# Deferred first loads, a fourth buffer for transposed inputs, and later normalization-factor transfers in a one-core transformer block

## The chip, the cores and the metric

The kernel runs on one core of one Trainium2 chip. The metric is device time in microseconds (us): the median of three runs. A profiled execution of the same program is used to see where the time goes; its span is the time from the first to the last instruction on the core.

## The reference

Sixteen sequences of 256 tokens with 256 channels, all float32, go through one pre-norm block: attention with 16 heads of 16 channels, then a gated feed-forward layer whose weights are interpolated from control points.

```python
x = x + attn(layernorm(x), wq, wk, wv, wo)
x = x + ffn(layernorm(x), gate_cp, up_cp, down_cp)

# attn: q, k, v = x @ w.T, split in 16 heads
scores = q k^T / sqrt(16); scores = -inf where j - i > 16
out = softmax(scores) v;   return out @ wo.T
# ffn: the weights are Catmull-Rom splines through 2033 control points each
return (silu(x @ gate_w.T) * (x @ up_w.T)) @ down_w.T
```

A query therefore sees every earlier token and 16 later ones.

## The kernel before

**Engines and order.** The kernel writes the order of the instructions of each engine out by hand: the wrapper `InOrder` (line 78) keeps each engine's queue in program order. TensorE (PE) multiplies, VectorE (DVE) takes maxima, products and statistics, ScalarE (ACT) exponentials and copies, GpSimd (POOL) masks and the power of -1/2. Nearly all transfers are issued by SyncE (SP), whose queue is in order too: an issue that waits for a buffer, an operand or an earlier transfer holds up every issue behind it. ACT issues the loads of the weights and, for batch 0, half of `spread`.

**A pipeline over the batches.** The loop at line 694 has 20 steps, s = 0 to 19. In step s, batch s-1 gets the maxima of its scores (`nb`), batch s-2 its exponentials and values (`tb`), batch s-3 the division, output projection and second normalization (`ob`), and batch s-4 most of its feed-forward layer. A step is cut into seven gaps, between which the scores of four head groups run (`inner` for groups 0 to 3 of the larger part, `outer` for the rest). `fill` puts feed-forward work in the gaps, `project` the work for a batch ahead: from step 4 on by a fixed rule, in steps 0 to 3 by the dictionary `early`, whose key is (step, gap) and whose value lists stages with their batch. In these steps the feed-forward weights are also made: `part` i builds one half of gate, up or down from `cp_in`, `tab_in` and `second_in`, and `keep_running` n issues n multiplications of the identity that nothing uses.

**The stages of a batch b that matter here.**

- `load_x(b)` and `load_xT(b)` load the batch's input as tokens by channels and as channels by tokens. x has ten buffers (pool `sbx`), xT three (`sb3`), each released after `project_v(b)`.
- `stats_a(b)` gives the factor 1/std of every token in `rstda`, 128 partitions by 2. `send_factors(b)` writes it to DRAM (`ra<-rstda`, 1 KB); `spread_factors(b)` reads it back to all partitions (`fa<-ra`, 128 KB), and so waits until the first has landed. Below they are ra(b) and fa(b).
- `project_qk(b)` multiplies xT by wq and wk into two PSUM buffers of the pool `ps_m`, which has two; DVE multiplies by fa(b) into `qkc`, which frees them. `spread(b)` lays qkc out over partitions by heads with eight transfers (`qk<-qkc`, 64 KB each). Batch 0 is normalized beforehand and needs no factors.
- `project_v(b)` does the same for the values, with `rstda` as ACT's scale.
- `turn_max(b)` sends the maxima of the scores to a row of qk with four transfers (`qk<-mxT`), which the scores for the exponentials need in the next step.
- `gather(b)` and `invert(b)` take the softmax sums and the heads back (`den<-au`, `ac<-au`), invert the sums on DVE (`rec`) and spread the inverses through DRAM (`rd<-rec`, `rb<-rd`).

**Initial loads.** Lines 139 to 158 issue, on SP, x0, x1, tab_in, cp_in 0, x2, xT1, second_in, cp_in 1, xT2, x3 and cp_in 2, and on ACT wq, wk, wv and wo. In every step lines 703 to 706, between gaps 1 and 2, issue x of batch s+4 and xT of batch s+3 (x4 and xT3 in step 0).

Of the kernel before, what the change touches and what calls it, by code (L numbers as in the profile page):

```python
# [11 lines left out]
F32 = mybir.dt.float32  # L12
# [6 lines left out]
P = 128  # L19
B, S, DIM = 16, 256, 256  # L20
# [73 lines left out]
def block_kernel(  # L94
# [14 lines left out]
    pe, dve, act, pool, sp = (  # L109
        InOrder(tc, e) for e in (nc.tensor, nc.vector, nc.scalar, nc.gpsimd, nc.sync)  # L110
    )

    const = ctx.enter_context(tc.tile_pool(name="const", bufs=1))
    sb = ctx.enter_context(tc.tile_pool(name="sb", bufs=2))
    sb1 = ctx.enter_context(tc.tile_pool(name="sb1", bufs=1))
    sb3 = ctx.enter_context(tc.tile_pool(name="sb3", bufs=3))
    sb4 = ctx.enter_context(tc.tile_pool(name="sb4", bufs=4))
# [10 lines left out]
    def load_x(b):  # L128
        xs[b] = sbx.tile([P, 2, DIM], F32, tag="x", name=f"x{b}")
        sp.dma_start(xs[b], x[b].rearrange("(c p) d -> p c d", p=P))  # L130


    xTs = {}

    def load_xT(b):
        xTs[b] = sb3.tile([P, 2, S], F32, tag="xT", name=f"xT{b}")
        sp.dma_start(xTs[b], xT[b].rearrange("(kc p) t -> p kc t", p=P))

    AHEAD = 2
    load_x(0)  # L140
    w_in = {}
    for nm, src in (("q", wqT), ("k", wkT), ("v", wvT), ("o", woT)):
        t = const.tile([P, 2, DIM], F32, tag=f"w{nm}", name=f"w{nm}")
        act.dma_start(t, src.rearrange("(kc p) o -> p kc o", p=P))
        w_in[nm] = t
    load_x(1)
    tab_in = const.tile([P, NPART + 2 * P], F32, tag="tab", name="tab_in")
    sp.dma_start(tab_in, tab)
    cp_in = const.tile([P, 3, NPART], F32, tag="cp", name="cp_in")
    second_in = const.tile([P, 2, NROW], mybir.dt.uint8, tag="second", name="second_in")  # L150
    sp.dma_start(cp_in[:, 0, :], cps[0])
    load_x(2)
    load_xT(1)
    sp.dma_start(second_in, second)
    sp.dma_start(cp_in[:, 1, :], cps[1])
    load_xT(2)
    load_x(3)
    sp.dma_start(cp_in[:, 2, :], cps[2])


    ident = const.tile([P, P], F32, tag="ident", name="ident")
# [53 lines left out]
    def normed(b, nm, tag):  # L215
        mv, rstd = moments.pop((b, nm))
        xn = sb.tile([P, 2, DIM], F32, tag=f"xn{tag}", name=f"xn{nm}{b}")
        for c in range(2):
            dve.tensor_scalar(
                xn[:, c, :], xs[b][:, c, :], mv[:, c, 0:1], rstd[:, c : c + 1],  # L220
                ALU.subtract, ALU.mult,
            )
        return xn

    def transposed(src, dst, nm):

        pt = ps_m.tile([P, 2, S], F32, tag="m", name=f"p{nm}")
        for kc in range(2):
            for c in range(2):
                pe.transpose(  # L230
                    pt[:, kc, c * P : (c + 1) * P],
                    src[:, c, kc * P : (kc + 1) * P],
                    ident,
                )
        act.copy(dst, pt)
# [6 lines left out]


    def norm_first():
        xTs[0] = sb3.tile([P, 2, S], F32, tag="xT", name="xT0")
        transposed(normed(0, "a", "f"), xTs[0], "ta0")

    sums = {}
# [119 lines left out]
    def inner(nb, tb, g):  # L368
        has_n, has_t = 0 <= nb < B, 0 <= tb < B
        qn, qt = qks[nb % NQK], qks[tb % NQK]  # L370
        if has_n:
            if g == 0:
                mxs[nb] = sb.tile([P, 2, H], F32, tag="mx", name=f"mx{nb}")
            scores(qn, True, g, P, S, P + HB + LOOK)
        if has_t:
            scores(qt, False, g, HB, HB - LOOK, S - HB + LOOK)
        if has_n:
            scores(qn, True, g, P + HB, S, S)
        if has_t:
            scores(qt, False, g, 0, 0, S)  # L380
        def exponentials(pr):
            e = sb6.tile([P, 2, S], F32, tag="e0", name=f"e0{tb}_{g}_{pr}")
            act.activation(e, tiles[pr][:, :, 0:S], AF.Exp, scale=HD**-0.5)

            pool.affine_select(
                out=e[:, :, 0:M0], in_=e[:, :, 0:M0],
                compare_op=ALU.is_ge, fill=0.0, base=LOOK,
                pattern=[[0, 2], [1, M0]], channel_multiplier=-1,
            )
            es[tb, 0, g, pr] = e  # L390

        def maxima(pr):
            for r in (2 * pr, 2 * pr + 1):
                find_max(nb, g, r, 1, S, S)

        read(exponentials if has_t else None, maxima if has_n else None)
# [205 lines left out]
    def do(stage, b, *args):  # L602
        if 0 <= b < B:
            stage(b, *args)
# [8 lines left out]
    def fill(s, gap):  # L613


        alone = s > B
        late = s >= B - AHEAD
        for what, at in (
            ((gate_up, s - 4, 1), 1),
            ((gate_up, s - 4, 2), 2 if late else 3),  # L620
            ((gate_up, s - 4, 3), 3 if late else 4),
            ((down, s - 4, 0), 4 if alone else 5),
            ((down, s - 4, 1), 5 if alone else 6),
            ((gate_up, s - 3, 0), 7),
        ):
            if at == gap:
                do(*what)
# [4 lines left out]
    def part(i):  # L632
# [7 lines left out]
        ),  # L640
        (0, 6): (
            (project_v, 0), (sum_weights, "v"), (center, "k"), (center, "v"), (keep_running, 1),
            (spread_factors, 1), (send_factors, 2), (spread_factors, 2),
        ),
        (1, 1): ((part, 0), (coefficients, 1)),
        (1, 2): ((project_qk, 1), (spread, 1)),
# [2 lines left out]
        (1, 5): ((keep_running, 2), (part, 2)),  # L649
        (1, 6): ((keep_running, 5), (project_v, 1)),  # L650
        (1, 7): (
            (stats_a, 3), (send_factors, 3), (spread_factors, 3), (keep_running, 4),
            (project_v, 2), (keep_running, 1),
        ),
        (2, 1): ((part, 3), (stats_a, 4), (send_factors, 4), (scores_and_values, 4)),
        (2, 2): ((project_qk, 3), (spread, 3), (spread_factors, 4)),
        (2, 3): ((keep_running, 6), (part, 4)),
        (2, 5): ((keep_running, 1), (part, 5)),
        (2, 6): ((keep_running, 4), (project_v, 3)),
        (2, 7): ((stats_a, 5), (send_factors, 5), (spread_factors, 5), (project_qk, 4)),  # L660
        (3, 1): ((stats_a, 6),),
        (3, 2): ((spread, 4), (project_qk, 5), (spread, 5), (send_factors, 6)),
        (3, 3): ((keep_running, 5), (project_v, 4)),
        (3, 4): ((spread_factors, 6),),
        (3, 6): ((keep_running, 4), (project_v, 5)),
    }
# [1 line left out]
    def project(s, gap):  # L668
        if s < 4:
            for stage, what in early.get((s, gap), ()):  # L670
                stage(what)
            return
        pb = s + AHEAD
        for stage, b, at in (
            (stats_a, pb + 1, 1),
            (project_qk, pb, 2),
            (spread, pb, 2),
            (send_factors, pb + 1, 2),
            (spread_factors, pb + 1, 4),
            (project_v, pb, 6),  # L680
        ):
            if at == gap:
                do(stage, b)
# [7 lines left out]
    stats_a(0)  # L691
    sum_weights("q")
    norm_first()
    for s in range(B + 4):
        nb, tb, ob = s - 1, s - 2, s - 3
        inner(nb, tb, 0)
        do(values, ob, 1)
        do(gather, ob)
        project(s, 1)
        fill(s, 1)  # L700
        inner(nb, tb, 1)
        do(invert, ob)
        if s + 2 + AHEAD < B:
            load_x(s + 2 + AHEAD)
        if 3 <= s + 1 + AHEAD < B:
            load_xT(s + 1 + AHEAD)
        project(s, 2)
        fill(s, 2)
        outer(nb, tb, 0)
        project(s, 3)  # L710
        fill(s, 3)
        inner(nb, tb, 2)
        do(values, tb, 0)
        project(s, 4)
        do(divide, ob)
        fill(s, 4)
        inner(nb, tb, 3)
        do(project_o, ob)
        do(stats_f, ob)
        project(s, 5)  # L720
        fill(s, 5)
        do(norm_f, ob)
        outer(nb, tb, 1)
        fill(s, 6)
        if s == 3:
            project(s, 6)
        do(turn_f, ob)
        if s != 3:
            project(s, 6)
        do(turn_max, nb)  # L730
        project(s, 7)
        fill(s, 7)
# [30 lines left out]
```

## Time and profile before

| | |
|---|---|
| median of three runs | 707.67 us (706.46 to 708.76) |
| the profiled execution: time, and span | 708.78 us, 707.0 us |
| mean granted TensorE clock | 0.958 |
| PE busy | 669.8 us, 95% of the span |
| DVE busy | 368.9 us, 52% |
| ACT busy | 208.2 us, 29% |
| POOL busy | 126.9 us, 18% |
| moved by DMA | 35.56 MB, mean 50 GB/s |

The page of the profile divides the span into 40 slices and gives each engine's busy share in tenths, the TensorE clock that was granted, and the load of the 16 DMA engines. The view of waits tells for how long an engine (or SP's queue) stood still and what ended it. The timeline lists start, duration and name of the instructions in order of time, with "x8" for eight merged ones. The table of stretches gives busy times, clock and DMA load between two times. All operations are recorded at one line, 88, so they are told apart by the names of their tiles, out<-in; batch numbers are left out and follow from the order.

### The profile page before, as it was taken

The numbers are of one execution on the slowest core, as the hardware profiler recorded it, in microseconds if no ns is written. First come the engines' busy times: TensorE is split into PE (matmuls) and PEld (weight loads), VectorE is DVE, ScalarE is ACT, GpSimd is POOL, SyncE is SP. The second block draws the span as 40 slices with busy tenths as digits, with TensorE's granted clock in tenths as the row PEclk, the third lists the DMA queues.
The fourth block names the chain that finished last, engine by engine and source line by source line (L and its number), as shares of the span: only waits on it lengthen the run. The fifth ranks groups of instructions, "written<-read, shape, count | busy, mean of one in ns | idle before, by whom it ended". The sixth has DMA issues, their size and how long they took to land.

```text
span 707.0 us, 18506 instructions
## 1 busy us (share of the span) xinstructions
PE 669.8 (95%) x7422; PEld 518.4 (73%) x7422; DVE 368.9 (52%) x1479; ACT 208.2 (29%) x368; POOL 126.9 (18%) x251
## 2 busy tenths in 40 slices
PE   7695997799999999999999999999999999999998
PEld 7363575478777777778787877777787777777777
DVE  5363455364665656465646566564637474633332
ACT  1021332232323333333323232333333233332210
POOL 5101221121121211121112111121212121211000
PEclk9695797799999999999999999999999999999999
DMA  9323505122131313141312214131201010100100
GB/s 256 46 51 45 76 4 110 30 73 43 39 63 32 79 33 85 27 91 26 85 32 69 48 24 77 31 67 33 54 19 33 20 30 25 27 26 24 40 22 16
DMA packets 44741, 35.56 MB, mean 50 GB/s; under 512 B 12400, under 2 KB 44016, under 8 KB 44656
## 3 DMA queue, kind: packets, MB, share of 16 engines
q1 hardware_dynamic: 43248, 33.07, 21.2%
q10 hardware_dynamic: 1408, 1.31, 1.2%
q8 instruction: 59, 0.97, 0.7%
q14 instruction: 26, 0.21, 0.2%
HBM read 16.78 MB, written 4.47 MB: 30 GB/s over the span
## 4 chain that ended last, share of the span: by engine, by line
PE 82%; DMA 2%; ACT 1%; SPq 1%; DVE 1%; issue 0%; ACTq 0%; DVEq 0%
PE pg L88 17%; PE pd L88 16%; PE pu L88 15%; PE scores L88 13%; PE po L88 6%; PE py L88 4%; PE pq L88 3%; PE pv L88 3%; PE pk L88 3%; SPq L88 1%; DMA ra<-rstda 1%; PE ptf L88 1%; ACT e L88 1%; DMA qk<-mxT 1%; ACT x2T L88 0%
## 5 line engine op out<-in xcount | busy, mean ns | idle before, releaser
L88 ACT ACTIVATE e<-scores 128x512 f32<-128x512 f32 (+1 forms) x192 | 117.7, 616 | 313.3 <-PE scores L88 238.2
L88 DVE CUSTOM_DVE_ANT_0 z<-scores,mask 128x144 bf16<-128x144 f32 (+1 forms) x512 | 154.5, 362 | 68.7 <-PE scores L88 60.3
L88 POOL TENSOR_SCALAR_AFFINE_SELECT e<-e 128x224 f32<-128x224 f32 (+1 forms) x192 | 93.3, 487 | 448.6 <-ACT e L88 448.2
L88 PE MATMUL scores<-qk 17*64 17x144 f32 (+7 forms) x4096 | 113.8, 329 | 21.5 <-DMA qk<-mxT 10.4
L88 PE MATMUL pg<-x2T,gateT 128*128 128x256 f32 x512 | 127.4, 392 | 2.9 <-ACT x2T L88 2.8
L88 PE MATMUL pu<-x2T,upT 128*128 128x256 f32 x512 | 121.8, 381 | 0.0
L88 PEld LDWEIGHTS scores<-qk 17*64 17x64 f32 (+1 forms) x4096 | 72.1, 135 | 61.9 <-issue 38.5
L88 PE MATMUL pd<-downT,inter 128*128 128x256 f32 x512 | 117.0, 382 | 0.0
L88 DVE SCALAR_TENSOR_TENSOR th<-th,pg 128x512 f32<-128x512 f32 x64 | 44.0, 688 | 132.3 <-ACT th L88 132.3
L88 PEld LDWEIGHTS pg<-x2T,gateT 128*128 128x128 f32 x512 | 93.1, 191 | 24.1 <-DVE mx L88 5.0
L88 PEld LDWEIGHTS pu<-x2T,upT 128*128 128x128 f32 x512 | 98.0, 191 | 13.6
L88 PEld LDWEIGHTS pd<-downT,inter 128*128 128x128 f32 x512 | 96.1, 190 | 14.0 <-issue 0.2
L88 ACT ACTIVATE th<-pg 128x512 f32<-128x512 f32 x64 | 38.3, 598 | 70.6 <-PE pg L88 70.2
L88 DVE TENSOR_TENSOR inter<-th,pu 128x512 f32<-128x512 f32 x64 | 44.1, 689 | 26.9 <-PE pu L88 26.9
L88 PE MATMUL po<-e,v 128*32 128x256 f32 (+1 forms) x1024 | 54.0, 355 | 0.0
L88 PEld LDWEIGHTS po<-e,v 128*32 128x32 f32 x1024 | 30.9, 115 | 26.4 <-issue 16.1
L88 DVE DVE_READ_ACCUMULATOR2_ANT mx<- 128x1 f32 x512 | 42.6, 83 | 0.1
L88 DVE TENSOR_TENSOR x<-x,pd 128x256 f32<-128x256 f32 x32 | 13.5, 422 | 51.1 <-PE pd L88 51.1
L88 PE MATMUL pq<-xT,wq 128*128 128x256 f32 x128 | 35.5, 425 | 1.4 <-ACT v L88 0.7
L88 PE MATMUL pv<-wv,xT 128*128 128x256 f32 x128 | 32.3, 397 | 3.6 <-DVE qkc L88 3.6
L88 PEld LDWEIGHTS pq<-xT,wq 128*128 128x128 f32 x128 | 25.2, 207 | 11.2 <-issue 4.4
L88 PE MATMUL pk<-xT,wk 128*128 128x256 f32 x128 | 31.8, 393 | 0.0
(67 smaller groups left out, 395.3 us busy)
## 6 DMA issues: line engine op xcount, KB each, us to landing
qk<-qkc SPq DMA_DIRECT2D x124, 64.0 KB
x<-x SPq DMA_DIRECT2D x16, 256.0 KB
ac<-au SPq DMA_DIRECT2D x128, 32.0 KB
rb<-rd SPq DMA_DIRECT2D x32, 128.0 KB
xT<-xT SPq DMA_DIRECT2D x15, 256.0 KB
out<-x SPq DMA_DIRECT2D x15, 256.0 KB
fa<-ra SPq DMA_DIRECT2D x15, 128.0 KB
qk<-mxT SPq DMA_DIRECT2D x64, 4.0 KB
```

The lines of the kernel that those rows point to most:

```text
L88: return self.tc.keep_in_program_order(fn(*args, **kwargs))
```

## The change

The transposed inputs move from the pool with three buffers to one with four (`sb4`). Before the loop only x0, x1, x2, tab_in, cp_in 0 and the weights wq, wk and wv are loaded. The other loads are in `load_rest`, whose two parts stand in step 0, gap 6, behind `spread(0)`: part 0 has xT1, second_in, cp_in 1 and xT2; part 1, behind fa(1) and ra(2), has cp_in 2, x3, x4, xT3 and wo, the last now on SP. The loop's loads begin in step 1. fa(3) moves from behind ra(3) in step 1 to the head of step 2, gap 2; fa(5) from behind ra(5) in step 2 to the head of step 3, gap 2. In step 3 `project_v(4)` moves from gap 3 to gap 2, `project_qk(5)`, `spread(5)` and ra(6) from gap 2 to gap 3, and five unused multiplications become three.

```diff
 def load_xT(b):
-    xTs[b] = sb3.tile([P, 2, S], F32, tag="xT", name=f"xT{b}")
+    xTs[b] = sb4.tile([P, 2, S], F32, tag="xT", name=f"xT{b}")
     sp.dma_start(xTs[b], xT[b].rearrange("(kc p) t -> p kc t", p=P))
...
-for nm, src in (("q", wqT), ("k", wkT), ("v", wvT), ("o", woT)):
-    t = const.tile([P, 2, DIM], F32, tag=f"w{nm}", name=f"w{nm}")
-    act.dma_start(t, src.rearrange("(kc p) o -> p kc o", p=P))
-    w_in[nm] = t
+def load_weight(nm, src, engine):
+    w_in[nm] = const.tile([P, 2, DIM], F32, tag=f"w{nm}", name=f"w{nm}")
+    engine.dma_start(w_in[nm], src.rearrange("(kc p) o -> p kc o", p=P))
+
+for nm, src in (("q", wqT), ("k", wkT), ("v", wvT)):
+    load_weight(nm, src, act)
...
 load_x(2)
-load_xT(1)
-sp.dma_start(second_in, second)
-sp.dma_start(cp_in[:, 1, :], cps[1])
-load_xT(2)
-load_x(3)
-sp.dma_start(cp_in[:, 2, :], cps[2])
+def load_rest(i):
+    if i == 0:
+        load_xT(1)
+        sp.dma_start(second_in, second)
+        sp.dma_start(cp_in[:, 1, :], cps[1])
+        load_xT(2)
+    else:
+        sp.dma_start(cp_in[:, 2, :], cps[2])
+        for b in (3, 4):
+            load_x(b)
+        load_xT(3)
+        load_weight("o", woT, sp)
...
 def norm_first():
-    xTs[0] = sb3.tile([P, 2, S], F32, tag="xT", name="xT0")
+    xTs[0] = sb4.tile([P, 2, S], F32, tag="xT", name="xT0")
...
 (0, 6): (
     (project_v, 0), (sum_weights, "v"), (center, "k"), (center, "v"), (keep_running, 1),
-    (spread_factors, 1), (send_factors, 2), (spread_factors, 2),
+    (load_rest, 0), (spread_factors, 1), (send_factors, 2), (load_rest, 1),
+    (spread_factors, 2),
 ),
...
 (1, 7): (
-    (stats_a, 3), (send_factors, 3), (spread_factors, 3), (keep_running, 4),
+    (stats_a, 3), (send_factors, 3), (keep_running, 4),
     (project_v, 2), (keep_running, 1),
 ),
 (2, 1): ((part, 3), (stats_a, 4), (send_factors, 4), (scores_and_values, 4)),
-(2, 2): ((project_qk, 3), (spread, 3), (spread_factors, 4)),
+(2, 2): ((spread_factors, 3), (project_qk, 3), (spread, 3), (spread_factors, 4)),
...
-(2, 7): ((stats_a, 5), (send_factors, 5), (spread_factors, 5), (project_qk, 4)),
+(2, 7): ((stats_a, 5), (send_factors, 5), (project_qk, 4)),
 (3, 1): ((stats_a, 6),),
-(3, 2): ((spread, 4), (project_qk, 5), (spread, 5), (send_factors, 6)),
-(3, 3): ((keep_running, 5), (project_v, 4)),
+(3, 2): ((spread_factors, 5), (spread, 4), (project_v, 4), (keep_running, 3)),
+(3, 3): ((project_qk, 5), (spread, 5), (send_factors, 6)),
 (3, 4): ((spread_factors, 6),),
...
-if s + 2 + AHEAD < B:
-    load_x(s + 2 + AHEAD)
-if 3 <= s + 1 + AHEAD < B:
-    load_xT(s + 1 + AHEAD)
+if s:
+    do(load_x, s + 2 + AHEAD)
+    do(load_xT, s + 1 + AHEAD)
```

## Prediction

> **What bounds the kernel now.** I read the page's slices first, to see where the time is lost.
>
> ```profile
> PE   7695997799999999999999999999999999999998
> PEclk9695797799999999999999999999999999999999
> DMA  9323505122131313141312214131201010100100
> ```
>
> A slice is 17.7 us. From the ninth on TensorE is busy at full clock. All loss lies in the first eight: gaps, and half clock after them. By the table of stretches, PE is busy 346.30 of 346.30 us from 185.8 to 532.1: a microsecond won in the first 140 reaches the end, and none is to be won later. (So the whole effect is a shift of step 4.)
>
> Then the waits up to 146 us, PE's own:
>
> ```profile
> PE scores L88 <- DMA qk<-mxT: 10.4, 2, 7.1
> PE scores L88 <- DMA qk<-qkc: 8.3, 3, 7.6
> PE pv L88 <- DVE qkc L88: 3.6, 1, 3.6
> ```
>
> Four gaps, by the timeline: 7.6 us to 23.76, 7.1 to 61.14, 3.6 to 109.86, 3.2 to 137.63: 21.5 in all. In six stretches behind or around them (20.4, 54.4, 78.6, 109.0, 129.4, 136.2 us) the granted clock is 0.50; they sum to 56.4 us with PE busy 43.39, so at full clock up to 21.7 us less.
>
> Three of the gaps end on DMAs of SyncE's queue and the other on a DVE product behind one, so I ask what that queue waited for (0 to 140 us: total, times, longest):
>
> ```profile
> SPq L88 <- DMA ra<-rstda: 30.6, 5, 8.4
> SPq L88 <- PE pm L88: 15.4, 1, 15.4
> ...
> SPq L88 <- DMA x<-x: 5.3, 1, 5.3
> SPq L88 <- PE pv L88: 3.8, 1, 3.8
> SPq L88 <- DMA wq<-wqT: 2.1, 1, 2.1
> ```
>
> and its timeline (start, us):
>
> ```profile
> 10.44 0.37 SPq L88 DMA_DIRECT2D ra<-rstda  x1
> ...
> 15.15 0.37 SPq L88 DMA_DIRECT2D xT<-xT  x1
> 15.62 8.12 SPq L88 DMA_DIRECT2D qk<-qkc  x4
> 23.84 0.53 SPq L88 DMA_DIRECT2D fa<-ra  x1
> 24.47 0.38 SPq L88 DMA_DIRECT2D ra<-rstda  x1
> 32.47 0.33 SPq L88 DMA_DIRECT2D fa<-ra  x1
> 32.86 0.43 SPq L88 DMA_DIRECT2D x<-x  x1
> 48.52 0.37 SPq L88 DMA_DIRECT2D xT<-xT  x1
> 49.00 10.24 SPq L88 DMA_DIRECT2D qk<-qkc  x16
> 59.34 2.33 SPq L88 DMA_DIRECT2D qk<-mxT  x4
> ```
>
> Gap 2: xT4 waits 15.4 us for a buffer (PE's project_v(1)); spread(1), whose operand was ready at 35.4, stands behind it, and mxT(0), ready at 49.67, behind 16 spreads, until 59.34. Gap 3: fa(5) waits at the queue's head for ra(5) (95.12 to 103.60); gather(0) is behind it, the reciprocal on DVE behind that, qkc(5) behind the reciprocal. Gap 4: fa(6) waits 6.7 us, mxT(2) behind it. Gap 1: spread(0) is ready at 13.1 and lands only after ra(1), at 22.2.
>
> **What the Trainium skill says.** "DMA: Bandwidth & Descriptors", Queues, rings and completion order: a DMA's semaphore is a strongly ordered write and counts only after every earlier write of that engine. The trace agrees: by its semaphore records ra(1), issued at 10.44, lands at 22.20, and x4, issued just behind it, at 22.36, though the queues moved only 10 to 73 GB/s between 16 and 22 us (stretches of one microsecond). So an ra delays all behind it. Same page, Two DMAs through the same engine are not ordered: the issuer must wait for the first before a dependent second; these are SyncE's 30.6 us. "TensorE: Matmul & The Clock Gate", The HAM clock gate: half rate after an idle window of about 3.4 us; here 0.50 appears 4.2 us after PE goes idle at 16.2, but also with gaps of 1.8 us (129.4).
>
> Prices from the records: ra 8.5 us from issue on idle queues (95.12 to 103.59), at least 5.6 after the landing before it; fa 4.4 (32.47 to 36.77); a spread issue 0.64, landing 2 later; mxT's first 1.6. Transfers wait for the landing of the eighth before them (the ninth, x2, waits 2.1 us for wq).
>
> **The change, part by part.**
>
> *Loads behind spread(0).* Ahead of spread(0) stay x0 to x2, wq, wk, wv, tab, cp0: 2.2 MB instead of 4.6, at 360 GB/s done near 9 us. ra(1) is still ahead, issued when rstda is ready (9.55), landing near 18.2; spread(0) is issued at 13.2 and counts just after it, group 0 near 19.0. PE restarts at 19.0 for 23.76: **4.7 us** gained. The load gone from ACT (wo, 0.49) joins SP's five of load_rest(1) (0.47 each), none of them needed before 30. The loads that were in step 0's loop body, x4 and xT3, are in that list; from step 1 on the loop issues the same two in the same place.
>
> *New wait, fa(2).* The eight-back rule holds load_rest(0) until spread(0) lands: xT1 is issued at 18.4, second, cp1, xT2, fa(1), ra(2) by 20.7. xT1 lands near 21 (latency 2.6) and is wanted near 22 (19.0 + scores 0.7 + pw 1.3 + gateT copies 1.1); second 0.6 us late for DVE; fa(1) 24. ra(2) lands at max(20.7+8.5, 24+5.6) = 29.5; then fa(2) is issued, behind cp2, x3, x4, xT3, wo, landing at 33.9. PE at full clock (four projections of 1.9 and scores 0.7 more) has pq(2), pk(2) done at 30 and soon needs a PSUM buffer that qkc(2) frees. qkc(2), coefficients(2), the maxima of group 2 (1.4+0.7+1.4): group 3's scores at 37.4 for 41.75. Gain there 4.3; the clock saved ahead is eaten by this wait.
>
> *Fourth xT buffer.* xT4 waits for nothing. spread(1) issues from 30.9, spread(2) from 36 to 41, and mxT(0), ready at 45.4 by PE's order (6.6 us from group 3 to pm, 1.4 to the copy), lands at 47.0. PE reaches step 2 at 37.4+6.6+3.4 = 47.4, no wait: 47.5 for 61.14. **Gain 13.6.**
>
> *fa(3) behind ra(4).* ra(3) goes at 47.8 and lands at 56.4. spread_factors(3) now follows ra(4), x6 and xT5: ra(4) needs stats_a(4), which follows step 2's first maxima and the predicated copies of upT, 6.7 us into the step by the rows at full clock (7.8 before): ready at 54.2, it lands at 62.7, and fa(3), issued at 56.5, counts after it, 63.1 (15.6 us into the step; before 75.50, 14.4 into it). Behind fa(3): spread(3), fa(4), mxT(1), none urgent. qkc(3) ends at 64.5, and group 2's scores follow 2.0 later as they did (77.2 to 79.17): 66.5. **Gain falls to 12.7**; step 2's faster clock is spent waiting.
>
> *fa(5) behind gather(0).* Step 3 starts at 83.1 (95.81). ra(5) lands 7.8 into it as before. den is issued at once but counts behind ra(5), at 91.3; reciprocal done at 92 instead of 109.2. So gap 3 as it was is gone: step 3's rows (scores 1.0, values 1.6, scores 1.2, pv(4) 1.9, runs 0.8, outer scores 1.5, pq(5) and pk(5) 3.8, group 2 1.2) run to 96. But fa(5) is now behind rd, four ac, two rb, x7 and xT6: before, xT6 landed 10.5 us after the reciprocal, and fa(5) lands 0.5 to 1 after that, near 103.3. values(1,0) needs the PSUM buffer of pq(5): it starts at 104.2 for 115.35. **Gain 11.1.** What comes next on SP, spread(4), hides under this wait; spread(5) goes 104.9 to 110.5.
>
> *ra(6), mxT(2).* ra(6) lands near 117.5, fa(6), then mxT(2), ready near 119.5, landing by 122. PE needs it 19.0 after values, later if half clock outlasts py and project_v(5); I add 2.3 (py 1.9, next 0.4): 125.5. Gap 4 is gone: 125.5 for 137.63, **12.1**. The two keep_running passes fewer are 0.55 us, beside waits, so nothing. Step 4's half clock from 136.2 (scores 1.82, po 2.90, pg 2.39 against 1.04, 1.56, 1.99) costs 2.5, mostly saved: +2.
>
> Sum: 14 us. Against the profiled execution, 708.78 (span 707.0 plus 1.8), 694.8; the median of the runs is 707.67, 1.1 lower: **694**.
>
> Unknown, from both sides: fa(2) lands between 31.5 and 36 (+2.4, -2.1 us); fa(3) +2, -2; fa(5) +4 (earlier rb), -3; the clock, which no view can place after new gaps of 2, 6 and 7 us, +5, -5. No bound under nothing for the buffer: it adds no instruction. Roots of squares give about 7: 687 to 701 for this case.
>
> **The rivals.**
>
> *More gain*: the fa waits lie under other work and the clock holds. Most of the 21.5 us of gaps and half of the 21.7 of clock: some 30 us, 678. For: the landings rest on few samples. Against: fa(3) and fa(5) are moved behind longer queues.
>
> *The wait moves on (no change)*: SP waits for fa(2) instead of xT4 with spread(1) behind it. It would need fa(2) to be issued near 44, and I have 29.5. 707.
>
> *Slower*: fa(5) in step 3. Its place behind seventeen transfers (8 of gather, rd, 4 ac, 2 rb, x7, xT6) prices it at 7 us now; PE, idle, stays at half clock. It decides when fa(5) lands over 14 us later than 103.3, near 118, so that all is given back; 16.5 later gives 710. For: each lane needs a landing eight back, and an ra in front delays every one. Against: the nine that follow the reciprocal took 10.5 us before; the eight ahead of it had an ra before them then too.
>
> **How the numbers follow.** Likeliest 0.74; more gain 0.15; no change 0.04; slower 0.07. About 0.3%, 2 us, is what a measurement can tell from no change. Faster 0.89, same 0.04, slower 0.07. The range takes the likeliest's and half of the gaining side: 683 to 702.
>
> **What would show it.** Right: no wait of xT on SP; PE's 7.1 us at step 2 gone; step 1's scores near 19; SP's fa(2) near 29.5; DVE waiting for fa three times, the longest in step 3. Wrong: scores of step 1 after 22, mxT(0) later than PE, or den landing long after 92.

## The result, and the profile after

| | before | after |
|---|---|---|
| median of 20 runs each | 708.89 us | 706.26 us (702.73 to 713.44) |
| ratio of the times | | 0.9963, 95% interval 0.9942 to 0.9983 |
| the profiled execution: time, and span | 708.78, 707.0 us | 707.75, 706.0 us |
| mean granted TensorE clock | 0.958 | 0.969 |

The change gains 2.6 us by the medians, where 14 were predicted. In the page's slices of the kernel after (17.65 us each, tenths of busy time, granted clock, DMA load) the loss has moved and not gone:

```profile
PE   7788693899999999999999999999999999999998
PEclk9969697899999999999999999999999999999999
DMA  5751304232221313041312214131201010010100
```

The second and the fourth slice have become better (6 to 7, 5 to 8). The fifth (71 to 88 us) has fallen from 9 to 6 and the seventh (106 to 124) from 7 to 3, and the third, at 8, now runs at 0.6 of the clock. The gaps at the fifth and the seventh are new places.

To see where each microsecond goes I divide the front of both traces at the same PE instructions: the first scores of step 1; `pm` (the turned maxima, at each step's end); `po` (the values) in the middle of steps 2 and 3 and at the head of step 4; and the `pm` of step 4. Behind that last one both kernels need the same 532 us to the end.

| stage, us | before | after | difference |
|---|---|---|---|
| to the first scores of step 1 | 23.76 | 18.39 | -5.4 |
| step 1, to pm(0) | 24.57 | 34.60 | +10.0 |
| to the values in step 2 (with what was gap 2) | 32.63 | 29.02 | -3.6 |
| to pm(1) | 10.11 | 10.24 | +0.1 |
| to the values in step 3 (with what was gap 3) | 24.28 | 28.59 | +4.3 |
| to pm(2) | 12.64 | 12.27 | -0.4 |
| to the values of step 4 (with what was gap 4) | 11.39 | 6.78 | -4.6 |
| to pm(3) | 35.47 | 33.74 | -1.7 |
| to the end | 532.2 | 532.4 | +0.2 |

Unrounded, the sum is -1.0, the difference of the two spans. One execution isn't the kernel: in two runs below that load as the kernel before does (e1, e9) the first scores of step 1 come at 21.35 and 22.36, so 1.4 to 2.4 us of the first line are this trace of before. The waits of PE up to 150 us (total, times, longest) name the new gaps:

```profile
PE po L88 <- DVE qkc L88: 11.0, 1, 11.0
PE pw L88 <- DVE qkc L88: 6.8, 2, 3.5
PE pw L88 <- remote: 3.8, 1, 3.8
PE pq L88 <- DMA xT<-xT: 2.7, 1, 2.7
```

No line `scores <- qk<-mxT` is left: gaps 2 and 4 are gone. All of the first two lines is waiting for a product `qkc` that frees a PSUM buffer. DVE's timeline shows what such a product waited for in step 2, and PE's timeline how long PE waits for one in step 3:

```profile
76.89 0.69 DVE L88 TENSOR_TENSOR qkc<-pq,fa 128x512 f32<-128x512 f32 x1 [13.45 <-DMA fa<-ra]
```

```profile
120.83 2.89 PE L88 MATMUL po<-e,v 128*32 128x256 f32 x32 [11.01 <-DVE qkc L88]
```

SP's waits (0 to 140 us) show that the change does to the queue what it says. The 15.4 us for the buffer of xT4 (`PE pm`) are gone, and the waits for an ra are halved from 30.6:

```profile
SPq L88 <- ACT mxT L88: 14.6, 2, 8.9
SPq L88 <- DMA ra<-rstda: 14.5, 4, 6.4
SPq L88 <- DVE mx L88: 14.2, 3, 12.7
SPq L88 <- POOL rstda L88: 10.3, 2, 5.6
```

So SP waits for ra less than half as long, and PE waits for fa longer than before. The factors are late for another reason than SP's standing still. SP's timeline around fa(2):

```profile
21.39 0.50 SPq L88 DMA_DIRECT2D ra<-rstda  x1
21.93 1.14 SPq L88 DMA_DIRECT2D cp_in<-cps  x1
23.12 1.65 SPq L88 DMA_DIRECT2D x<-x  x2
25.03 0.37 SPq L88 DMA_DIRECT2D xT<-xT  x1
25.71 0.37 SPq L88 DMA_DIRECT2D wo<-woT  x1
30.96 0.34 SPq L88 DMA_DIRECT2D fa<-ra  x1
```

All of `load_rest(1)`, 1.3 MB, is issued by 26.1, five microseconds before fa(2). The table of stretches (us; PE, PEld, DVE, ACT, POOL busy; clock; DMA share, which counts each packet where it starts and so can pass 1; GB/s) shows what becomes of it:

```profile
22.00:24.00 2.00, 0.00 (x0) 0.00 (x0) 0.00 (x0) 0.00 (x0) 0.00 (x0) 1.00 0.99 348
24.00:26.00 2.00, 1.50 (x5) 1.23 (x6) 0.87 (x2) 0.00 (x0) 0.00 (x0) 0.72 1.77 277
26.00:30.00 4.00, 4.00 (x26) 3.07 (x31) 3.10 (x12) 0.00 (x0) 0.00 (x0) 0.71 0.46 45
30.00:33.00 3.00, 3.00 (x44) 2.52 (x36) 2.52 (x17) 0.00 (x0) 0.00 (x0) 1.00 0.47 95
33.00:36.00 3.00, 3.00 (x29) 1.90 (x28) 0.00 (x0) 0.00 (x0) 0.00 (x0) 1.00 0.93 230
```

ra(2) lands at 30.90. From 26 us on the queues move 45 and then 95 GB/s, though by the packet records some 0.9 of the 1.3 MB behind ra(2) has still to go; 348 and 277 moved before, and 230 follow. By the semaphore records x4 lands at 34.1, xT3 at 35.6, wo at 36.6 and fa(2), behind all of them, at 38.86. An ra of 1 KB seems to slow the queues that it lies in; the experiments have to show it.

### The profile page after: what moved, and what is told of

It reads as the page before. It is cut to its first block, busy times and chain, and to the rows that moved or that the text cites. A ratio compares the mean times of both kernels' runs of the same rounds, so it can differ in the third digit from the quotient of the medians.

```text
span 706.0 us, 18505 instructions
## 1 busy us (share of the span) xinstructions
PE 663.7 (94%) x7418; PEld 514.7 (73%) x7418; DVE 368.6 (52%) x1479; ACT 208.1 (29%) x368; POOL 126.8 (18%) x251
## 5 line engine op out<-in xcount | busy, mean ns | idle before, releaser
L88 PE MATMUL scores<-qk 17*64 17x144 f32 (+7 forms) x4096 | 109.4, 322 | 5.7 <-DMA qk<-qkc 2.3
L88 PEld LDWEIGHTS scores<-qk 17*64 17x64 f32 (+1 forms) x4096 | 70.6, 133 | 44.7 <-issue 31.5
L88 PEld LDWEIGHTS po<-e,v 128*32 128x32 f32 x1024 | 30.6, 113 | 35.8 <-issue 25.4
L88 PE MATMUL pq<-xT,wq 128*128 128x256 f32 x128 | 33.3, 405 | 4.1 <-DMA xT<-xT 2.7
L88 PE MATMUL py<-wo,ac 128*128 128x256 f32 x128 | 31.8, 391 | 0.0
```

Source lines behind the costliest of these rows:

```text
L88: return self.tc.keep_in_program_order(fn(*args, **kwargs))
```

## The experiments

Theory A: the places are to blame. Each fa stands behind a list that it need not stand behind, and SP's waits pass from xT4 to it. Theory B: ra itself is to blame. It is slow, the transfers behind it stand nearly still, and much of what the change puts between an ra and its fa moves only after it. Ratios are to the kernel before on the same chip, with the 95% interval; single traces of one kernel differ more than these, so stages and ratios are read together. In the short diffs `-` and `+` are against the kernel after if nothing else is said.

**What the buffer is worth.**

*e1, the buffer alone*

```diff
 # against the kernel before: nothing but the pool
-    xTs[b] = sb3.tile(...)      # and xTs[0]
+    xTs[b] = sb4.tile(...)
```

> The kernel before with the fourth xT buffer and nothing else. Theory (waits behind factor transfers gave the gain back): the wait of 15.4 us on SP for xT4's buffer goes, spread(1) starts near 35.5 instead of 49.0, step 2's main scores come near 52 instead of 61.1, and since fa(3) and fa(5) stay where they were, most of it reaches the end: 8 to 12 us less than before, 697 to 701. Rival (the buffer's wait was covered, or half clock takes the gain): within 3 us of before, 705 to 709.

Measured: 696.76 us, 0.9884 (0.9842 to 0.9925). The stage with gap 2 falls from 32.63 to 22.06, mxT(0) is issued at 47.42 for 59.34, and gap 4 stays:

```profile
PE scores L88 <- DMA qk<-mxT: 6.6, 1, 6.6
```

The buffer alone gains three times what the whole change gains: the rest of the change costs more than it brings.

*e8, everything but the buffer*

```diff
-    xTs[b] = sb4.tile(...)      # and xTs[0]
+    xTs[b] = sb3.tile(...)
```

> The changed kernel with three xT buffers again. Theory: xT4 waits on SP for project_v(1), both spreads and mxT(0) behind it, so step 2 starts 6 to 9 us later relative to step 1's end: 4 to 9 us more than the changed kernel. Rival (spreads wait for fa(2) anyway, the buffer is worth nothing beside it): within 2 us.

Measured: 712.87 us, 1.0161 (1.0105 to 1.0216). SP's waits name the old one again:

```profile
SPq L88 <- PE pm L88: 19.3, 1, 19.3
```

and PE waits 7.0 for mxT; the stage to the values of step 2 takes 38.76 for 29.02. So without the buffer the change loses, and the buffer is worth 2% inside it, some 14 us, more than the 4 to 9 expected.

**The places of fa, one by one.**

*e4, fa(2) ahead of the loads*

```diff
-            (load_rest, 0), (spread_factors, 1), (send_factors, 2), (load_rest, 1),
-            (spread_factors, 2),
+            (load_rest, 0), (spread_factors, 1), (send_factors, 2), (spread_factors, 2),
+            (load_rest, 1),
```

> The changed kernel with fa(2) ahead of load_rest(1) (cp2, x3, x4, xT3, wo). Theory: ra(2) still lands near 31, but fa(2) lands 4.4 us later, near 35.3, instead of 38.9 behind 1.3 MB that crawled behind ra(2); step 1 ends 3 to 5 us sooner (part of it clock): 701 to 703 if it carries. Rival (a later wait, for fa(3), takes it): step 1 sooner, total within 1.5 us of the changed kernel.

Measured: 700.67 us, 0.9953 (0.9925 to 0.9981). fa(2) is issued at 28.88, as soon as ra(2) has landed (28.86), and lands at 34.24 for 38.86. Step 1 takes 28.80 us for 34.60. The interval overlaps that of the kernel after, and not all of the 5.8 us is the edit's: three kernels of this study with steps 0 and 1 as in the kernel after (e2, e3, e8) have fa(2) at 35.0 to 36.3 and step 1 at 31.2 to 32.0. Two kernels further down that move fa(2) too have the step at 29.40 and 30.97 (e7, e10), so by the means of three the place is worth about 2 (29.7 for 31.7), and by the ratios under 1: the rival, that a later wait takes it, came nearer. The step is still 4 longer than before the change, of which 2.6 is half clock, though PE waited only 0.85 us ahead of it: from group 3's scores (37.68) to pm(0) 9.2 us, where e1 has 6.6.

*e2, fa(3) ahead of ra(4)*

```diff
-        (2, 1): ((part, 3), (stats_a, 4), (send_factors, 4), ...),
-        (2, 2): ((spread_factors, 3), (project_qk, 3), ...),
+        (2, 1): ((part, 3), (stats_a, 4), (spread_factors, 3), (send_factors, 4), ...),
+        (2, 2): ((project_qk, 3), ...),
```

> The changed kernel with fa(3) issued ahead of ra(4) again. Theory: fa(3) lands 4.5 us after ra(3), near 70, instead of 76.8 behind ra(4) and x6; group 2's scores of step 2 come near 74.5 instead of 80.2, so 4 to 6 us less than the changed kernel, 700 to 702. Rival (the clock, not fa(3), sets step 2; or the next wait, for fa(5), takes it all): under 1.5 us.

Measured: 698.1 us, 0.9916 (0.9884 to 0.9949). fa(3) lands at 66.30 for 76.77, and the stage takes 22.19 us, as in e1 (22.06). The place behind ra(4) costs 6.8 us in this stage; by the ratios (0.9916 beside 0.9963) some 3 us of it reach the end.

*e3, fa(5) straight behind the gather's first half*

```diff
-        (3, 1): ((stats_a, 6),),
-        (3, 2): ((spread_factors, 5), (spread, 4), ...),
+        (3, 1): ((spread_factors, 5), (stats_a, 6)),
+        (3, 2): ((spread, 4), ...),
```

> The changed kernel with fa(5) directly behind gather(0) instead of behind rd, four ac, two rb, x7 and xT6. Theory: fa(5) is issued near 106.6 and lands near 111.3 instead of 119.9; PE's wait of 11.0 us before the values of step 3 falls to about 3, less what the output projection then waits for rb: 6 to 8 us less than the changed kernel, 698 to 700. Rival (the wait moves on to rb and the division): under 3 us.

Measured: 703.55 us, 0.9989 (0.9969 to 1.0008), so no gain. PE's waits up to 150 us:

```profile
...
PE scores L88 <- DMA qk<-mxT: 3.1, 1, 3.1
PE py L88 <- issue: 2.5, 1, 2.5
...
PE po L88 <- DVE qkc L88: 1.7, 1, 1.7
```

fa(5) is there (issued 104.84, landed 108.95), and the wait of 11.0 ahead of the values is 1.7. The stage falls from 28.59 to 18.80. But fa(6) now waits at the queue's head until 131.72, with mxT(2) behind it: the two stages that follow take 26.8 for 19.1, so of 9.8 us gained 7.7 are given back to what was gap 4. The rest goes in half clock, which in this execution lasts to pm(1) (13.2 for 10.2). The wait goes from one fa to the next.

*e7, fa(2) and fa(3)*

```diff
 # the edits of the two kernels with fa(2) and fa(3) first, together
```

> The changed kernel with fa(2) ahead of load_rest(1) and fa(3) ahead of ra(4). Theory: the two gains lie in different steps (fa(2) in step 1, 3 to 5 us; fa(3) in step 2, 6 to 7 us) and add: 9 to 12 us less than the changed kernel, ratio to before 0.980 to 0.985. Rival (fa(5)'s wait in step 3 takes what comes early): ratio 0.990 or more.

Measured: 696.8 us, 0.9906 (0.9888 to 0.9924). By stages both gains are there (29.40 and 22.52), and the span of the profiled execution is 694.4; the ratio gains less than their sum, as the rival has it. With both places mended the change is where the buffer alone is.

*e10, all four fa*

```diff
 # fa(2), fa(3), fa(5) moved as above, and
-        (3, 4): ((spread_factors, 6),),
+        (3, 7): ((spread_factors, 6),),      # behind mxT(2)
```

> The changed kernel with fa(2) ahead of load_rest(1), fa(3) ahead of ra(4), fa(5) behind gather(0) and fa(6) behind mxT(2). Theory: fa(5) wins 8 us in step 3, of which the wait for rb and the division takes 2 to 4, and the wait for mxT that took the rest in the run with fa(5) alone is gone: 3 to 6 us less than with fa(2) and fa(3) alone, ratio to before 0.982 to 0.986. Rival (the division takes all): ratio 0.989 or more.

Measured: 691.1 us, 0.9821 (0.9749 to 0.9894). All four places mended, step 1 is still at 30.97 us, and the stage behind pm(0) at 22.19.

*e9, the buffer and fa(6)*

```diff
 # against the kernel before: the buffer, and
-        (3, 4): ((spread_factors, 6),),
+        (3, 7): ((spread_factors, 6),),
```

> The kernel before with the fourth xT buffer, and fa(6) behind mxT(2) instead of ahead of it. Theory: gap 4 (6.6 us of waiting for mxT in the run with the buffer alone) was SP standing at fa(6) with mxT(2) behind it; it goes, and nothing takes its place: 5 to 7 us less than with the buffer alone, ratio to before 0.978 to 0.981. Rival (fa(6), later, makes queries and keys of batch 6 late in step 4): ratio 0.986 or more.

Measured: 689.51 us, 0.979 (0.9729 to 0.985). Two edits to the kernel before do as well as the whole change with all its places mended. Theory A explains steps 2 and 3, not step 1, and no net gain from the deferred loads is seen: what they win ahead of step 1 is lost in it.

**The transfer itself.**

*e5, no ra*

```diff
-        sp.dma_start(across[b].rearrange("(c p) -> p c", p=P), factors[b])
...
-        sp.dma_start(to, across[b].unsqueeze(0).to_broadcast([P, S]))
+        sp.dma_start(to, tab[4, 0:S].unsqueeze(0).to_broadcast([P, S]))
```

> The changed kernel without the writes of the factors to DRAM (no ra); every fa reads 256 fixed numbers of the table instead, so queries and keys get wrong factors. SP no longer waits for an ra and no ra stands in the queues. Theory (an ra both holds SP and delays all that is queued behind it): PE's waits for qkc(2), qkc(3) and qkc(5), 3.3, 7.4 and 11.0 us, nearly vanish, with them most half clock: 18 to 25 us less than the changed kernel, 682 to 688. Rival (the waits for fa come from the length of the queue and from half clock): under 8 us.

Measured: 677.47 us, 0.9633 (0.9604 to 0.9661). Step 1 takes 21.59 us and the next stage 15.78. Only fa(5)'s place is left among the large waits of PE:

```profile
PE po L88 <- DVE qkc L88: 7.3, 1, 7.3
```

*e6, ra unread*

```diff
 # ra is written as in the kernel after, and nothing reads it
-        sp.dma_start(to, across[b].unsqueeze(0).to_broadcast([P, S]))
+        sp.dma_start(to, tab[4, 0:S].unsqueeze(0).to_broadcast([P, S]))
```

> As the run without ra, but every ra is still written, in its place, and read by nobody: SP never waits for one, the queues still carry them. Theory (what is queued behind an ra counts only after it): fa(2), fa(3) and fa(5) land little sooner than in the changed kernel, since each has an ra ahead of it: 2 to 6 us less than the changed kernel. Rival (only SP's wait at the queue's head costs): as fast as the run without ra, within 3 us.

Measured: 700.13 us, 0.9952 (0.9932 to 0.9973). SP's timeline has no wait ahead of fa(2) any more:

```profile
20.87 1.37 SPq L88 DMA_DIRECT2D ra<-rstda  x1
...
24.83 0.44 SPq L88 DMA_DIRECT2D fa<-tab  x1
```

and fa(2) still lands only at 36.16, 11.3 us after its issue; step 1 takes 32.89. e5 and e6 differ by the writes alone, and by 23 us. So the writes cost what theory B says, not by SP's waiting for them (without it the kernel is 0.1% faster by the ratios) but by what lies behind them in the DMA queues.

*e12, ra in runs of 8 bytes*

```diff
-        sp.dma_start(across[b].rearrange("(c p) -> p c", p=P), factors[b])
+        sp.dma_start(across[b].rearrange("(p c) -> p c", p=P), factors[b])
```

> The changed kernel with an ra written in the partitions' order, as 128 runs of 8 bytes instead of 256 of 4; the factors come back in another order than the tokens', so queries and keys get wrong ones. Theory (an ra's time goes with the number of its runs): it lands 4.5 to 6 us after its issue on idle queues instead of 8.5, and the total falls by 5 to 12 us. Rival (a fixed time of a write to DRAM): 8 to 8.5 us as before, total within 2 us of the changed kernel.

Measured: 684.89 us, 0.9722 (0.9652 to 0.9791). The same 1 KB goes in 128 runs of 8 bytes in place of 256 of 4. ra lands 2.8 to 3.0 us after its issue (9.60 to 12.63; 77.32 to 80.13 in step 2), not 8.5, and faster than the 4.5 to 6 expected of half as many runs. Step 1 takes 24.98, as before the change.

*e13, fewer runs*

```diff
 # 128 runs of 4 bytes: one column of rstda, read twice
+        sp.dma_start(across[b][0:P].unsqueeze(1), factors[b][:, 0:1])
```

> The changed kernel with an ra of 128 runs of 4 bytes: only the factors of a batch's first 128 tokens are written, and used for its other 128 too. If the number of runs sets an ra's time, it lands 3 to 5 us after its issue on idle queues, as the 128 runs of 8 bytes did (2.8 to 3.0). If the size of a run sets it (4 bytes against 8), it lands 6 to 8.5 us after.

Measured, one time: 701.83 us beside 703.74 of the kernel before. ra takes 8.2 us (9.24 to 17.45) and 6.8 (90.87 to 97.65); step 1 takes 32.72.

*e14, more and longer runs*

```diff
 # 256 runs of 8 bytes: the pair of moments of every token
+        across[b] = dr.tile([2 * S], F32, tag="ra", name=f"ra{b}")
+        sp.dma_start(across[b].rearrange("(c p k) -> p c k", p=P, k=2), mv)
```

> The changed kernel with an ra of 256 runs of 8 bytes: the mean and variance of every token are written instead of the factor, and the first 256 of these numbers are used as factors. If the number of runs sets an ra's time: 8 us or more. If their size does: 3 to 4.5 us.

Measured, one time: 689.21 us. ra takes 3.1 us (8.54 to 11.64) and 2.7 (80.90 to 83.59). Half as many runs of 4 bytes are nearly as slow as all, and the full number of runs of 8 bytes is fast. So it is the size of a run, not their number. (All these runs lie side by side in DRAM; runs of 4 bytes that lie apart were not tried.)

*e15, 8 bytes, read with a stride*

```diff
+        sp.dma_start(across[b].rearrange("(p c) -> p c", p=P), factors[b])
...
-    qkc[:, i], pq, across[b].unsqueeze(1).to_broadcast([P, 2, S]), ALU.mult
+    qkc[:, i].rearrange("q o (c p) -> q o c p", c=2),
+    pq.rearrange("q o (c p) -> q o c p", c=2),
+    across[b].rearrange("q (p c) -> q c p", c=2).unsqueeze(1).to_broadcast([P, 2, 2, P]),
+    ALU.mult,
```

> The changed kernel with an ra in 128 runs of 8 bytes, and DVE reading the factors back in the tokens' order with a stride of two, so that every query and key gets its own factor. Theory: DVE's products take the same 0.69 us or little more, and the total is that of the 8-byte run, ratio to before 0.970 to 0.976 (the change then brings more than the 14 us that were predicted). Rival (the strided read costs DVE enough to show): 0.98 or more.

Measured: 685.39 us, 0.9767 (0.9716 to 0.9819). DVE's product reads its factors with a stride of two and takes 0.69 us as it did. SP's timeline around fa(2), for 21.39 and 30.96 in the kernel after:

```profile
19.42 0.38 SPq L88 DMA_DIRECT2D ra<-rstda  x1
...
24.88 0.34 SPq L88 DMA_DIRECT2D fa<-ra  x1
```

*e11, ra(2) early*

```diff
 # with the four places mended, and ra in its runs of 4 bytes
-        (0, 1): ((stats_a, 1), (send_factors, 1)),
+        (0, 1): ((stats_a, 1), (send_factors, 1), (stats_a, 2), (send_factors, 2)),
...                                        # and out of their old places
```

> As the last, and ra(2) written straight behind ra(1), ahead of spread(0). Theory: both ra overlap and fa(2) lands near 26 instead of 33, so step 1 takes 22 to 25 us instead of 29; step 1 itself starts 0 to 4 us later, since spread(0) counts only after ra(2): 1 to 5 us less than the last. Rival (two ra in a row take 5.6 us more, to 23, and hold all first loads): 0 to 3 us more.

Measured: 687.47 us, 0.9758 (0.9703 to 0.9813). ra(2) now runs beside ra(1), ahead of the loads (11.58 to 21.43). Step 1 takes 23.96 us, but its first scores come at 21.73 for 18.39, since spread(0) stands behind two ra. Beside e10 (17.97 and 30.97) the longer way to step 1 costs half of what the shorter step 1 brings.

**What is left of the change with a short ra.**

*e16, 8 bytes and all four fa*

```diff
 # the kernel with ra in 8 bytes, and fa(2), fa(3), fa(5), fa(6) moved as above
```

> As the last, with fa(2) ahead of load_rest(1), fa(3) ahead of ra(4), fa(5) behind gather(0) and fa(6) behind mxT(2). Theory: with a short ra the places of fa(2) and fa(3) matter little (up to 2 us), fa(5)'s still does (PE waits 7.2 us for it in the 8-byte run, behind loads and rb): 3 to 7 us less than the last. Rival (the division takes it): within 2 us.

Measured: 676.28 us, 0.9602 (0.956 to 0.9643). That is 12 us less than e15 by the ratios, more than the 3 to 7 expected: with a short ra the places still matter.

*e17, the kernel before with 8 bytes*

```diff
 # against the kernel before: ra in 8 bytes, and nothing else
```

> The kernel before with an ra in 128 runs of 8 bytes and the strided read on DVE; nothing of the change. Theory: gap 2 stays (it was xT4's buffer), gaps 3 and 4 (SP standing at a fa) shrink by 3 us each, gap 1 by some 3, with half clock: 8 to 14 us less than before, ratio 0.980 to 0.988; the change beside short factor transfers is then worth 3 to 8 us (0.9767 with it). Rival (the change is worth nothing once ra is short): 0.978 or less.

Measured: 689.17 us, 0.9792 (0.9776 to 0.9809). Gap 2 stays (7.1 us for mxT, 20.1 on SP for the buffer). Beside the same ra in the kernel after (e15, 0.9767) the whole change makes no difference that the intervals can tell. By the profiled executions it has won 2.9 us at the start of step 1 and 7.0 in the stage with gap 2 (22.04 for 28.99), and lost 6.6 in step 3, where fa(5) straight behind a short ra gives a stage of 17.44 us and behind the gather 24.06.

*e18, buffer, fa(6) and 8 bytes*

```diff
 # against the kernel before: ra in 8 bytes, the fourth buffer, and
-        (3, 4): ((spread_factors, 6),),
+        (3, 7): ((spread_factors, 6),),
```

> As the last, with the fourth xT buffer and fa(6) behind mxT(2). Theory: gap 2 goes too, 8 to 10 us less than the last, ratio 0.968 to 0.974; the deferred loads and fa(5) behind gather(0) are what the run with 8 bytes and all new places (0.9602) has beyond it. Rival (the loads are what counts at the start): 0.976 or more.

Measured: 670.58 us, 0.9534 (0.9513 to 0.9556), the fastest of all, 5% below the kernel before and by the ratios 4% below the kernel after, and twice the 8 to 10 us expected of these two edits. PE's largest waits up to 150 us:

```profile
PE scores L88 <- DMA qk<-qkc: 2.4, 1, 2.4
PE pm L88 <- ACT v L88: 1.8, 1, 1.8
```

Beside it e16, with the deferred loads and the other places, wins 1.9 us at the start (16.50 against 18.40) and loses 1.3 in step 1 and 6.3 in the stage behind it (22.07 against 15.79). There e16's PE waits 1.7 us for mxT(0) and runs at half clock from 46.9 to 57.1 us, where this kernel has full clock; its DVE doesn't wait for fa(3).

## Why the prediction was wrong, step by step

The mechanism held: each gap that was to go went, each new wait came where it was named, and the sign was right. The sizes failed, and the step that failed in two of them (fa(2) and fa(3)) is the price of ra. The prediction took it as a delay (8.5 us from issue) after which what is behind counts at once, the data having moved meanwhile. It quoted the 10 to 73 GB/s between 16 and 22 us as a sign that only landings are held; the same rates fit data that stand still, and it never asked which. The other step that failed is the clock behind the new wait.

- *Loads behind spread(0)*: 19.0 predicted, 18.39 measured. Right, though the 23.76 that it was set against is a late trace (21.35 and 22.36 in e1 and e9). What it loads later came late: xT1 landed at 24.37 for "near 21", fifteen of its sixteen parts by 22.41, and second_in kept DVE waiting 4.1 us where 0.6 was said.
- *fa(2)*: its issue was right (30.96 for 29.5), its landing not (38.86 for 33.9): the term "issued, behind cp2, x3, x4, xT3, wo, landing at 33.9" has five loads moving beside ra(2). Group 3's scores came at 42.49 for 37.4, **5.1 us** lost. Some 3 of it is this one execution, in which the last of fa(2)'s sixteen parts came 2.8 us behind the others; in e2, e3 and e8 the same scores come at 38.6 to 39.9, 1.2 to 2.5 late, and with fa(2) ahead of the loads (e4, e7, e10) at 36.6 to 37.8.
- *The clock* ("+5, -5" for all): "the clock saved ahead is eaten by this wait" has full clock behind the wait. Between 39 and 53 us it is 0.53, and group 3 to pm(0) takes 10.5 us where 6.6 were put (10.1 to 10.8 in e2, e3 and e8). **3.9 us** lost at this place alone. What sets the length of such a spell stays open: e7 and e8 have it behind waits of PE of 0.85 us.

```profile
39.00:53.00 14.00, 13.11 (x83) 8.08 (x84) 10.29 (x44) 1.66 (x3) 0.69 (x1) 0.53 0.37 56
```

- *Fourth buffer*: mechanism and size right (no wait on SP, no gap at step 2; the buffer alone shows it). Step 2 began at 56.29 for 47.5 by the two terms above.
- *fa(3)*: 15.6 us into the step predicted, 20.5 measured. ra(4) took 10.2 us (62.87 to 73.09), x6 and xT5 landed behind it at 75.7 and 76.4, fa(3) at 76.77. **4.9 us** lost, where ±2 was given.
- *fa(5)*: 20.2 us into step 3 predicted, 22.9 measured, and so another **2.7 us**, of which 1.6 is the last of its sixteen parts (118.31 and 119.88); PE waited 11.0 where about 7 were said. The rival "slower via fa(5)" has the place right, and fa(5) did land past its 118, but 13.9 of the 16.6 us were lost before step 3 began (96.99 for 83.1).
- *Gap 4*: gone, as said; mxT(2) landed at 137.77 and the scores of step 4 start at 138.91, 18.1 us behind the values where 21.3 were put: 3.2 us better. Step 4's clock gave 1.7 for 2.

5.1 + 3.9 + 4.9 + 2.7 - 3.2 is 13.4 us, step 4's scores at 138.91 for 125.5: the predicted gain of 14 is all but gone, and the spans show 1.0 (the medians 2.6). "No change: the wait moves on" came nearest to the truth; its mechanism (SP waiting for fa(2)) was not it. Much of the wait moved from SP's queue into the DMA queues. "DVE waiting for fa three times" is right, with 6.6, 13.4 and 12.1 us, but the longest is in step 2.

That ra's price is the whole of the miss is not shown. With a short ra in both kernels the change is still worth nothing that the intervals can tell (e15 and e17). In the traces of that pair the gaps that it was to close are smaller too (in e17 3.2 us for 7.6 at gap 1, none left of gaps 3 and 4), and fa(5)'s new place loses 6.6.

How such a step would have been sized: ask how many bytes lie between ra and the fa that is wanted, and how many of them have still to move when ra lands. By the packet records of fa(2)'s case 0.4 of the 1.3 MB had gone by 26.0 and 0.7 by 30.9; the rest with fa(2) itself, 0.75 MB, took until 36.05 (fifteen of sixteen parts), 5.1 us and not the 4.4 of an fa alone. To that comes half clock: between group 3 and pm(0) it cost 3.5 to 4.5 us in six kernels (after, e2, e3, e7, e8, e10) and 2.6 in e4.

Three slips of the prediction change nothing: max(20.7+8.5, 24+5.6) is 29.6, fa's 32.47 to 36.77 is 4.3 us, and the half clock of gap 1 begins at 20.16, 4.0 us after PE went idle.

On the fixed cost of a transfer the Trainium skill ("DMA: Bandwidth & Descriptors", Latency and other measured facts) speaks of about 2 us with the round trip to the memory as its largest part. The writes of 8 bytes agree roughly (2.6 to 3.1 from issue); those of 4 bytes don't (6.8 to 8.6), and there the measurement decides.

## What to carry to other kernels

Price a small transfer by the size of its runs and by the bytes queued between it and the transfer that is wanted; an issuing engine that waits less can leave its consumers waiting longer. Try the one edit that frees the head of a queue by itself before a reordering around it: here one buffer was worth 1.2%, and the moves beside it took most of that away. When three or four waits in a profile name the same small transfer, look at its shape first; one rearranged write was worth 2% in both kernels, where moving all four fa was worth 1.4% (e10 beside the kernel after) to 1.7% (e16 beside e15).

## What was not expected of the hardware

- A DRAM write of 128 or 256 runs of 4 bytes takes 6.8 to 8.6 us from issue on otherwise quiet queues, one of 128 or 256 runs of 8 bytes 2.6 to 3.1. With the loads of step 0 ahead of it the short one too needs 5.4 to 6.5 (19.42 to 24.81 in e15, 19.23 to 25.69 in e12).
- The difference arises at the end. All packets of the first ra are recorded by 10.6 us both in the kernel after (issued 9.49) and in e15 (9.54); its sixteen parts land from 14.92 to 18.08 in the one and from 10.78 to 12.14 in the other.
- While a write of 4-byte runs is under way, loads behind it move slowly: 45 and 95 GB/s in the kernel after, 33 to 40 from 26 to 30 us in e2, e3, e6 and e8. Why was not settled; no run here looked inside the DMA engines.
- Of the sixteen parts of a load one can be 2 to 3 us behind the others: in the kernel after fa(2)'s fifteenth landed at 36.05 and its last at 38.86. This is left open. Some such parts land shortly after a packet of 16 KB of the kind that the profile calls "instruction" (xT1's last at 24.37, the packet at 21.75), but fa(2)'s doesn't, and the records don't say which engine a packet used. The `remote` wait of 3.8 us that the profile shows inside step 2's long wait is open too.
